# Summing the scan's states two pairs late, with a ninth state buffer, split rings for B and C, smaller loads of u and y, and a reordered opening

## The chip, the cores and the metric

The kernel runs on one core of a Trainium2 chip, in fp32. The metric is the device time of one execution in microseconds. The core has five engines that work side by side, each from its own queue in order: TensorE (PE), VectorE (DVE), ScalarE (ACT), GpSimd (POOL) and SyncE (SP), which here issues the DMAs.

## The reference

A sequence model of four layers runs on two sequences (b = 0, 1) of 1024 positions with 256 channels. Layer 0 is a Mamba block whose normalisation is shifted, scaled and gated by rows made from a condition vector. Layer 1 is a block of the same kind with two state-space models, of which the second runs backwards in time. Layer 2 is a linear attention, layer 3 a softmax attention, both with a shift and scale from the condition (FiLM). Most of the time goes into the state-space models, 512 channels with 16 states each:

```
def step(h, inp):
    dt_t, B_t, C_t, u_t = inp
    dA = jnp.exp(dt_t[:, :, None] * A)
    h = h * dA + (dt_t * u_t)[:, :, None] * B_t[:, None, :]
    y = jnp.einsum('bdn,bn->bd', h, C_t)
    return (h, y)
...
_, ys = jax.lax.scan(step, h0, seq)
y = jnp.transpose(ys, (1, 0, 2)) + u * D_param
y = y * jax.nn.silu(z)
```

There are six such recurrences: one for each sequence in layer 0, two for each in layer 1.

## The kernel before, in words

The order of instructions is written out by hand: the order of the program is the order on each engine's queue, and the tile pools add the waits for data and for buffers.

**The scans.** `chain()` runs the six recurrences one after the other in the order s00, s01, s10, s20, s11, s21 (layer, model, sequence as the code counts them). A tile holds 32 channels x 4 states on the 128 partitions and all 1024 positions; one recurrence has 64 tiles. They are taken in pairs that share four states (index k of 0 to 3): four blocks d of 128 channels, two halves cp of 64 channels, four k. That is 192 pairs p and 384 tiles, 2p and 2p+1. A tile takes these steps:

- `decay` (L133 as `dA_t<-sp`): ACT computes exp(A dt) from a spread of dt (`sp0`: 32 rows repeated four times by a DMA) into PSUM.
- `inputs` (L936): POOL multiplies the spread of dt*u (`sp1`) by B (`bc`, four rows repeated over 32 channels) into a state buffer `hb_t`. There are 8 of these buffers.
- `tile` (L943 backwards, L947 forwards): DVE runs the scan; then the result is multiplied by C, on DVE (L950), or for 99 of the 384 tiles on POOL (L949, called through `rest()`), whenever a running balance of the two engines' work says so.
- `fold` (L974): PE sums the four states of every channel into a bank `ys_t` by four matmuls for each tile. At k = 0 `begin` (L960, L964) opens the bank with u*D, and with the other direction's y where there are two.
- `finish` (L982): after four pairs the bank is multiplied by the gate on DVE, or copied by ACT, and stored by DMA.

In pair p the instructions come in this order: POOL's product for tile 2p+3, ACT's decay for 2p+1, a slot of other work, DVE's tile 2p, at k = 2 the finish of the group before, the gate's load at k = 3, the decay for 2p+2, the product for 2p+4, POOL's multiplication by C if there is one, a second slot, DVE's tile 2p+1, and at the end PE's sums for pair p-1:

```
            if p:
                fold(p - 1)
        fold(len(pairs) - 1)
```

The DMAs of the scans all go through SP's queue: `load_spread` (L899) fetches the spreads for the next group of pairs, three buffers for `sp0` and three for `sp1`; `load_bc` (L889) fetches B and C for one k into one ring of eight buffers, and for the next recurrence it is issued behind each of the last four pairs; `load_rest` (L913) fetches u and y for 128 channels into single buffers and makes a diagonal matrix of D; `load_gate` fetches the gate by 64 channels in two halves.

**The other work.** Everything else that the layers need (normalisation, projections, rows from the condition, the closing projection of each layer, the linear attention, the start of layer 3) is a queue of steps, `Behind`. `behind.slot()` is called twice for each pair and takes as many steps as its credits allow. `cond_later` is one of these steps: it makes the shift, scale and gate rows of layer 1 for both sequences, with matmuls (L95) and four POOL operations for each sequence. `until()` runs steps at once when a load needs their result.

**The opening.** Before the scans, the first sequence's preparation runs in the open: normalisation (`refine`, `scaled`), transposes with an eviction that applies the affine rows (`channels`), the projection into u and z, convolution, the projection to dt, B and C, and then the loads of the first scan. At the end of the scans, the softmax attention runs, from about 1476 us to the end.

Of the kernel before, what the change touches and what calls it, by code (L numbers as in the profile page):

```python
# [18 lines left out]
P = 128  # L19
# [18 lines left out]
for _name, _n in (  # L38
    ("ln_g0", 2), ("ln_b0", 2), ("ada_b0", 4), ("conv_w", 16), ("conv_b", 4),
    ("dt_b0", 4), ("D0", 4), ("Alog0", 64),  # L40
    ("n2g", 2), ("n2b", 2), ("bx", 4), ("bz", 4), ("bc1", 4), ("bc2", 4),
    ("dt_b1", 4), ("dt_b2", 4), ("D1", 4), ("D2", 4), ("Alog1", 64), ("Alog2", 64),
    ("ng2", 2), ("nb2", 2), ("bk2", 2), ("bv2", 2), ("emb_b2", 4), ("fg2", 2), ("fb2", 2),
    ("ng3", 2), ("nb3", 2), ("bq3", 4), ("bk3", 4), ("emb_b3", 4), ("fg3", 2), ("fb3", 2),
    ("mask3", 16), ("bq3d", 2), ("bk3d", 2), ("ones3", 2),
):
    _COLS[_name] = (_NCOLS, _n)
    _NCOLS += _n
# [6 lines left out]
def kernel(ctx: ExitStack, tc: tile.TileContext, a: dict, out: bass.AP):  # L55
# [5 lines left out]
    hbp = ctx.enter_context(tc.tile_pool(name="hbp", bufs=8))  # L61
# [141 lines left out]
    nc.scalar.preload_act_table_set("natural_log_exp_and_others")  # L203
# [49 lines left out]
    def affine(mod, scale_at, shift_at, g, bias, name):  # L253

        s = const.tile([P, 2, B], F32, tag=f"{name}s", name=f"{name}s")
        o = const.tile([P, 2, B], F32, tag=f"{name}o", name=f"{name}o")
        for c in range(2):
            g_c, b_c = col(g, c), col(bias, c)
            at = mod[:, scale_at + c, :]
            act_f(s[:, c, :], at, AF.Identity, bias=g_c, scale=g_c)  # L260
            t = small_t((P, B), "aff")
            act_f(t, mod[:, shift_at + c, :], AF.Identity, bias=b_c)
            for b in range(B):
                act_f(
                    o[:, c, b : b + 1], at[:, b : b + 1], AF.Identity,
                    bias=t[:, b : b + 1], scale=b_c,
                )
        return s, o
# [34 lines left out]
    def cond_later():  # L303
        scb = spread_cond()
        brow = abuf((1, 3 * D))
        nc.sync.dma_start(brow, a["ada_row1"])
        w = load_k("ada_w1", 3 * D)
        g1 = abuf((P, 2, D))
        nc.sync.dma_start(g1[:, 0, :], a["norm1_g"].partition_broadcast(P))
        nc.sync.dma_start(g1[:, 1, :], a["norm1_b"].partition_broadcast(P))  # L310
        yield 5 * T
        made = []
        yield from pipe(*(
            cond_rows(w, scb, brow, i * D, b, f"{name}1_{b}", res)
            for b in range(B)
            for i, (name, res) in enumerate(
                (("shift", made), ("scale", made), ("gate", cond["gate1"]))
            )
        ))
        for b in range(B):  # L320
            o, s = made[2 * b : 2 * b + 2]
            t = small_t((P, 2, D), "t2", 1)[:, 0, :]
            nc.gpsimd.tensor_scalar(s, s, 1.0, None, ALU.add)
            nc.gpsimd.tensor_tensor(t, s, g1[:, 1, :], ALU.mult)
            nc.gpsimd.tensor_tensor(o, o, t, ALU.add)
            nc.gpsimd.tensor_tensor(s, s, g1[:, 0, :], ALU.mult)
            cond["s1"].append(s)
            cond["o1"].append(o)
            yield
# [95 lines left out]
    def scaled(src, r, q):  # L425
        o = abuf((P, 4, D))
        for j in range(4 if mode["tail"] else 0):
            nc.vector.tensor_scalar(
                o[:, j, :], src[:, j, :], r[:, j : j + 1], q[:, j : j + 1], ALU.mult, ALU.add
            )  # L430
        for j in range(0 if mode["tail"] else 4):
            act_f(
                o[:, j, :], src[:, j, :], AF.Identity,
                bias=q[:, j : j + 1], scale=r[:, j : j + 1],
            )
        return o

    def normed(src, res):

        mv = small_t((P, 4 * len(src), 2), "mv", 4)  # L440
        for i, t in enumerate(src):
            stats(t, mv[:, ts(i, 4), :])
            yield
        r = root(mv)
        yield mode["least"] * 3 // 2
        q = refine(mv, r)
        yield
        for i, t in enumerate(src):
            res.append(scaled(t, r[:, ts(i, 4)], q[:, ts(i, 4)]))
            yield  # L450
# [7 lines left out]
    def channels(src, dst, func, scale, bias, halves=(0, 1)):  # L458


        def turn(i, c):
            ps = bank()
            for j in range(4):
                flip(ps[:, ts(j, P)], src[halves.index(i)][:, j, ts(c, P)])
            return ps

        def take(i, c, ps):
            act_f(
                dst[c][:, ts(i, 512)], ps, AF.Identity, bias=bias(c), scale=scale(c)
            )  # L470

        yield from pipe(*(
            (lambda i=i, c=c: turn(i, c), lambda ps, i=i, c=c: take(i, c, ps))
            for i in halves for c in range(2)
        ))
        if func is AF.Silu:
            done = slice(512 * halves[0], 512 * halves[-1] + 512)
            act_f(dst[0][:, done], dst[0][:, done], func)
            silu(dst[1][:, done])
            yield  # L480
# [75 lines left out]
    def ssm_inputs(key, u, w_xp, w_dt, dt_b, st):  # L556
# [15 lines left out]
        if key == "00":  # L572
# [7 lines left out]
            take(0, pss[0])  # L580
            nc.vector.tensor_copy(dbl[:, 512:], pss[1][: R + 2 * N, :])
# [5 lines left out]
        save(2, st["bc"], dbl[R : R + 2 * N, :])  # L587

# [287 lines left out]
    class Scan:  # L876
# [8 lines left out]
        def load_bc(self, k):  # L885
            for w in range(2):
                t = bcp.tile([P, T], F32, tag="bc", name="bc")
                at = w * N + k * NS
                nc.sync.dma_start(  # L889
                    t,  # L890
                    self.st["bc"][at : at + NS, :].unsqueeze(0).to_broadcast([DS, NS, T]),
                )
                self.bc[w][k] = t

        def load_spread(self, c, w):

            behind.until(lambda: len(self.st["have"]) > c // 4)
            t = spread.tile([P, T], F32, tag=f"sp{w}", name=f"sp{w}")
# [7 lines left out]
        def load_rest(self, d):  # L906
# [3 lines left out]
            self.rest[d] = {"D": diag(col(self.Dp, d), "dgD")}  # L910
            for key, src in srcs.items():
                t = fin.tile([P, T], F32, tag=f"f{key}", name=f"f{key}")
                nc.sync.dma_start(t, src[ts(d, P), :])  # L913
                self.rest[d][key] = t
# [5 lines left out]
        def load_gate(self, d, cp):  # L920
            if self.gate:
# [4 lines left out]
                self.rest[d]["g"] = t  # L926
# [7 lines left out]
        def inputs(self, c, k):  # L934
            e = hb()
            nc.gpsimd.tensor_tensor(e, self.sp[c, 1], self.bc[0][k], ALU.mult)  # L936
# [15 lines left out]
        def begin(self, d, cp):  # L952
# [3 lines left out]
            rest = self.rest[d]  # L956
            r = ts(cp, 64)
            for ch in range(2):
                o = self.ys[d, cp][ts(ch, 64), :]
                nc.tensor.matmul(  # L960
                    o, rest["D"][r, r], rest["u"][r, ts(ch, 512)], start=True, stop=False
                )
                if self.add is not None:
                    nc.tensor.matmul(  # L964
                        o, ident[r, r], rest["y"][r, ts(ch, 512)], start=False, stop=False
# [13 lines left out]
        def finish(self, d, cp):  # L979
            t = yp.tile([P, 512], F32, tag="y", name="y")  # L980
            if self.gate:
                nc.vector.tensor_tensor(t, self.ys[d, cp], self.rest[d]["g"], ALU.mult)  # L982
# [8 lines left out]
    def chain(scans, rates, early, mid, after):  # L991
# [29 lines left out]
        for w in range(2):  # L1021
            s.load_spread(0, w)
        s.load_bc(0)
        for w in range(2):
            s.load_spread(1, w)
        for k in range(1, NK):
            s.load_bc(k)
        s.load_rest(0)
        ahead(0, "decay")
        ahead(0, "inputs")  # L1030
# [5 lines left out]
        for p, (i, d, cp, k) in enumerate(pairs):  # L1036
# [10 lines left out]
            if k == 2 and cp == 1:  # L1047
                if d < 3:
                    s.load_rest(d + 1)
                elif nxt:  # L1050
                    nxt[0].load_rest(0)
# [25 lines left out]
            if k == 2 and nxt:  # L1077
                nxt[0].load_spread(nxt[1] + 1, 0)
# [7 lines left out]
            if final and i + 1 < len(scans):  # L1086
                scans[i + 1].load_bc(k)

            if p:
                fold(p - 1)  # L1090
        fold(len(pairs) - 1)
# [36 lines left out]
    def layer2(b, src, dst):  # L1128
# [110 lines left out]
        at = small.tile([P, 2, P], F32, tag="at", name="at", bufs=1)  # L1239
# [158 lines left out]
    def attention(sts, done):  # L1398
# [24 lines left out]
        def top(n, step, j, ps):  # L1423
            t, ch = divmod(step, 2)
            if n not in mh:
                mh[n] = small.tile([P, NT, 2, 4], F32, tag="mh", name="mh", bufs=2)
# [88 lines left out]
    ctx.enter_context(tc.manual_schedule())  # L1515
    sts = [{"v": [], "qk": [], "y": []} for _ in range(B)]
    with ExitStack() as s:
        bcp, spread, fin, yp = [
            s.enter_context(tc.tile_pool(name=n, bufs=k))
            for n, k in (("bcp", 8), ("spread", 3), ("fin", 1), ("yp", 2))  # L1520
        ]
        psum.append(s.enter_context(tc.tile_pool(name="psS", bufs=1, space=bass.MemoryType.PSUM)))
        s00 = Scan("00", negA[0], "D0", False, True)
        s01 = Scan("01", negA[0], "D0", False, True)
# [70 lines left out]
        for _ in range(7):  # L1595
            behind.step()
        behind.add(
            cond_first(), cond_later(), p01, p10, p20, cond_last(), p11, p21,
# [12 lines left out]
    home[0] = ctx.enter_context(tc.tile_pool(name="act2", bufs=17))  # L1611
    psum.append(ctx.enter_context(tc.tile_pool(name="psA", bufs=1, space=bass.MemoryType.PSUM)))
# [11 lines left out]
def _layout(i):  # L1624
# [16 lines left out]

    def heads(v, const_at=None):
# [11 lines left out]
        "dt_b0": cols(f["L0_cond_dt_proj_b"]), "D0": cols(f["L0_cond_D_param"]),  # L1654
# [5 lines left out]
        "D1": cols(f["L1_cond_Dp1"]), "D2": cols(f["L1_cond_Dp2"]),  # L1660
# [59 lines left out]
```

## Time and profile before

| | |
|---|---|
| median of 3 runs | 2124.39 us (2119.06 to 2125.03) |
| time of the profiled execution | 2117.43 us, its span 2115.4 us |
| first scan on DVE starts | 69.51 us |
| PE busy | 1626.8 us (77%), weight loads 617.7 us |
| DVE busy | 1745.5 us (83%) |
| ACT busy | 1140.4 us (54%) |
| POOL busy | 1356.9 us (64%) |
| POOL's products L936 | 384 at 2399 ns, 908.8 us |
| DVE's scans and products of L943 to L950 | 2279 to 2287 ns a scan, 1225 ns a product by C |
| PE's sums L974 | 1536 matmuls, 294.2 us |

How to read it: the busy shares are averages over a stretch of scans and a stretch of attention, in which other engines are full. In the scans one has to ask which of DVE and POOL is idle, and for whom. In the lines of waits, the engine and the line that waited stand ahead of the arrow and what released them behind it, with the total in us, the number of times and the longest. `hb_t` is a state buffer: a wait of POOL at L936 for PE is a wait for a buffer to come free.

### The profile page before, as it was taken

What the parts mean: (1) busy time and instruction counts of PE and PEld (TensorE: products, weight loads), DVE (VectorE), ACT (ScalarE), POOL (GpSimd) and SP (SyncE); (2) the same over time, 40 slices, a digit from 0 to 9 for tenths busy, and PEclk for the clock granted to TensorE, in tenths of its full rate; (3) what the DMA queues carried; (4) which work ended last, traced back from release to release, by engine and by line L of the source; (5) the groups of instructions that cost most, each with busy time, mean ns of one, the idle gap of its engine ahead of it and who ended that gap; (6) DMA issues with size and microseconds to landing.
All of it is one profiled execution on the core that took longest, in us unless ns stands there. A gap on an engine that the chain in (4) does not pass through costs nothing.

```text
span 2115.4 us, 22775 instructions
## 1 busy us (share of the span) xinstructions
PE 1626.8 (77%) x8112; PEld 617.7 (29%) x8112; DVE 1745.5 (83%) x1728; ACT 1140.4 (54%) x1583; POOL 1356.9 (64%) x667
## 2 busy tenths in 40 slices
PE   6576867288697547886945658944999899999997
PEld 3132313033141202222312323300545333333333
DVE  4688898898999999998999987998767757777763
ACT  5565666375546345764555453542044555656665
POOL 0789898898999999999998977998101211000000
PEclk9688968599796558988977865965899999999999
DMA  3663458245653555555653344332300111020001
GB/s 111 239 222 114 157 184 292 83 157 185 254 196 141 179 172 187 189 179 188 250 206 110 117 159 144 123 132 73 116 1 1 39 21 18 23 56 1 2 1 38
DMA packets 106870, 267.53 MB, mean 126 GB/s; under 512 B 14618, under 2 KB 39067, under 8 KB 106756
## 3 DMA queue, kind: packets, MB, share of 16 engines
q1 hardware_dynamic: 106756, 266.07, 37.1%
q8 instruction: 64, 1.05, 0.2%
q14 instruction: 50, 0.41, 0.1%
HBM read 195.90 MB, written 67.90 MB: 125 GB/s over the span
## 4 chain that ended last, share of the span: by engine, by line
PE 30%; DVE 10%; POOL 5%; issue 4%; ACT 2%; DMA 0%; DVEq 0%; ACTq 0%; POOLq 0%
PE sc_t L1418 13%; PE av_t L1458 6%; PE sc_t L95 4%; POOL hb_t L936 3%; PE bank_t L95 3%; DVE dA_t L943 2%; DVE mh L1427 2%; PE sc_t L99 2%; DVE dA_t L947 2%; POOL hb_t L949 1%; PE ys_t L974 1%; DVE hb_t L943 1%; ACT act_t L133 1%; POOL act_t L141 1%; DVE hb_t L947 1%
## 5 line engine op out<-in xcount | busy, mean ns | idle before, releaser
L936 POOL TENSOR_TENSOR hb_t<-sp,bc 128x1024 f32<-128x1024 f32 x384 | 908.8, 2399 | 88.5 <-PE ys_t L974 52.0
L133 ACT ACTIVATE dA_t<-sp,negA 128x1024 f32<-128x1024 f32 x384 | 428.5, 1117 | 548.3 <-DVE hb_t L950 432.8
L947 DVE TENSOR_TENSOR_SCAN dA_t<-dA_t,hb_t 128x1024 f32<-128x1024 f32 x195 | 445.9, 2287 | 62.3 <-ACT dA_t L133 35.1
L1427 DVE TENSOR_REDUCE mh<-sc_t 128x1 f32<-128x512 f32 x512 | 327.5, 686 | 110.2 <-PE sc_t L1418 109.8
L974 PE MATMUL ys_t<-hb_t,fold 128*32 128x512 f32 x1536 | 294.2, 781 | 153.5 <-POOL hb_t L949 101.1
L133 ACT ACTIVATE hb_t<-sc_t 128x512 f32<-128x512 f32 x512 | 276.9, 595 | 188.7 <-PE sc_t L1418 188.5
L950 DVE TENSOR_TENSOR hb_t<-dA_t,bc 128x1024 f32<-128x1024 f32 x285 | 349.1, 1225 | 21.4 <-DVE dA_t L947 0.5
L1418 PE MATMUL sc_t<-act_t 32*128 32x512 f32 x2048 | 336.6, 650 | 11.0 <-DVE mh L1427 7.3
L949 POOL TENSOR_TENSOR hb_t<-hb_t,bc 128x1024 f32<-128x1024 f32 x99 | 235.7, 2381 | 19.6 <-DVE hb_t L947 17.8
L784 POOL TENSOR_TENSOR act_t<-act_t,row 128x1024 f32<-128x1024 f32 x8 | 18.7, 2347 | 339.9 <-PE sc_t L99 193.3
L943 DVE TENSOR_TENSOR_SCAN dA_t<-dA_t,hb_t 128x1024 f32<-128x1024 f32 x90 | 205.7, 2285 | 9.2 <-POOL hb_t L936 6.0
L1458 PE MATMUL av_t<-hb_t,act_t 128*32 128x256 f32 x2048 | 164.3, 393 | 1.1 <-DVE act_t L1466 1.1
L95 PE MATMUL bank_t<-act_t,w_c_w 128*128 128x512 f32 x256 | 129.6, 657 | 41.2 <-ACT act_t L133 41.2
L133 ACT ACTIVATE act_t<-bank_t,cols 128x512 f32<-128x512 f32 (+1 forms) x206 | 129.9, 677 | 44.5 <-PE bank_t L95 38.7
L1418 PEld LDWEIGHTS sc_t<-act_t 32*128 32x128 f32 x2048 | 111.1, 185 | 120.9 <-issue 79.9
L974 PEld LDWEIGHTS ys_t<-hb_t,fold 128*32 128x32 f32 x1536 | 40.5, 123 | 358.9 <-POOL hb_t L949 139.5
L947 DVE TENSOR_TENSOR_SCAN hb_t<-dA_t,hb_t 128x1024 f32<-128x1024 f32 x61 | 139.0, 2279 | 3.9 <-ACT dA_t L133 3.6
L141 POOL TENSOR_TENSOR act_t<-act_t 128x1024 f32<-128x1024 f32 x50 | 118.4, 2367 | 0.2
L99 PE MATMUL bank_t<-ident,act_t 128*128 128x128 f32 x128 | 34.6, 426 | 92.5 <-ACT act_t L133 92.3
L95 PE MATMUL bank_t<-act_t,w_dt_w 64*128 64x512 f32 x96 | 74.6, 912 | 40.4 <-ACT act_t L133 34.4
L1458 PEld LDWEIGHTS av_t<-hb_t,act_t 128*32 128x32 f32 x2048 | 42.1, 108 | 190.5 <-issue 177.8
L1363 POOL MEMSET act_t<- 128x1024 f32 x8 | 7.6, 952 | 128.0 <-PE sc_t L1418 128.0
(176 smaller groups left out, 1833.9 us busy)
## 6 DMA issues: line engine op xcount, KB each, us to landing
sp<-dt SPq DMA_DIRECT2D x192, 512.0 KB, 5.3
dt<-act_t SPq DMA_DIRECT2D x48, 512.0 KB, 5.2
bc<-bc SPq DMA_DIRECT2D x48, 512.0 KB, 7.7
u<-act_t SPq DMA_DIRECT2D x24, 512.0 KB, 5.0
fu<-u SPq DMA_DIRECT2D x24, 512.0 KB, 4.5
y<-y SPq DMA_DIRECT2D x96, 128.0 KB, 5.8
g<-act_t SPq DMA_DIRECT2D x16, 512.0 KB, 5.3
fg<-g SPq DMA_DIRECT2D x64, 128.0 KB, 4.7
```

What stands on the lines that cost most here:

```text
L95: nc.tensor.matmul(o, w, x, **kw)
L133: nc.scalar.activation(o, x, func, **kw)
L141: nc.gpsimd.tensor_tensor(o, x, y, op)
L936: nc.gpsimd.tensor_tensor(e, self.sp[c, 1], self.bc[0][k], ALU.mult)
L943: nc.vector.tensor_tensor_scan(h[:, ::-1], dA[:, ::-1], e[:, ::-1], 0.0, ALU.mult, ALU.add)
L947: nc.vector.tensor_tensor_scan(h, dA, e, 0.0, ALU.mult, ALU.add)
L949: return lambda: nc.gpsimd.tensor_tensor(e, h, self.bc[1][k], ALU.mult)
L950: nc.vector.tensor_tensor(e, h, self.bc[1][k], ALU.mult)
L974: nc.tensor.matmul(self.ys[d, cp][at : at + DS, :], fold, e[:, ts(ch, 512)], start=False, stop=(k == NK - 1),)
L1418: nc.tensor.matmul(ps, w[r, ts(at, P)], x[r, ts(wide_at, 512)], start=True, stop=True)
L1427: nc.vector.tensor_reduce(mh[n][:, t, ch, j : j + 1], ps, AX.X, ALU.max)
L1458: nc.tensor.matmul(sums.av[32 * j : 32 * j + 32, ts(part, 256)], sts[b]["v"][t // 2][:, t % 2, 4 * g + j, :], es[j // 2][:, at : at + 256] ...
```

## The change

- The sums of a pair come two pairs later instead of one, and there are 9 state buffers instead of 8.
- The spreads of dt have four buffers instead of three. The first spread for the second tile's channels is issued at k = 1 instead of k = 2.
- B and C have a ring of four buffers each. For the next recurrence, B is issued ahead of the pair's first product, C behind the second tile.
- u and y are loaded for 64 channels, in two halves of 64 partitions x 512 positions, at every k = 3; before, for 128 channels at k = 2 of every second group. The diagonal of D is made for 64 channels (48 instead of 24 times).
- `cond_later` is split by sequence: the part for the second sequence runs after the preparation of s20, with its own load of the weights.
- The opening: half of the scalings, the affine rows and the second half of the evictions go from ACT to DVE; the copies of the dt, B, C projection are both on DVE; the first B is loaded right behind its store; the first product is on DVE; the order of the first loads is changed; the activation table is asked for behind the start of the hand-written order.
- Two small tiles share other tiles' memory.

```diff
-    hbp = ctx.enter_context(tc.tile_pool(name="hbp", bufs=8))
+    hbp = ctx.enter_context(tc.tile_pool(name="hbp", bufs=9))
...
     act_f(sc, cT, AF.Silu)
-    nc.scalar.preload_act_table_set("natural_log_exp_and_others")
...
             at = mod[:, scale_at + c, :]
+            if not mode["scans"]:
+                t = small_t((P, B), "aff")
+                nc.vector.tensor_scalar(t, at, 1.0, None, ALU.add)
+                nc.vector.tensor_scalar(s[:, c, :], t, g_c, None, ALU.mult)
+                nc.vector.scalar_tensor_tensor(
+                    o[:, c, :], t, b_c, mod[:, shift_at + c, :], ALU.mult, ALU.add
+                )
+                continue
...
-    def cond_later():
+    def cond_later(b):
         scb = spread_cond()
         brow = abuf((1, 3 * D))
         nc.sync.dma_start(brow, a["ada_row1"])
...
-    def scaled(src, r, q):
+    def scaled(src, r, q, i):
         o = abuf((P, 4, D))
-        for j in range(4 if mode["tail"] else 0):
+        far = mode["tail"] or i and not mode["scans"]
+        for j in range(4 if far else 0):
...
         def take(i, c, ps):
+            if c and not (mode["scans"] or mode["tail"]):
+                nc.vector.tensor_scalar(
+                    dst[c][:, ts(i, 512)], ps, scale(c), bias(c), ALU.mult, ALU.add
+                )
+                return
...
         save(2, st["bc"], dbl[R : R + 2 * N, :])
+        if "first" in st:
+            later(2, st["first"])
...
-        def load_bc(self, k):
-            for w in range(2):
-                t = bcp.tile([P, T], F32, tag="bc", name="bc")
...
+        def load_bc(self, k, w):
+
+            t = bcp.tile([P, T], F32, tag=f"bc{w}", name=f"bc{w}")
...
-            t = spread.tile([P, T], F32, tag=f"sp{w}", name=f"sp{w}")
+            t = spread.tile([P, T], F32, tag=f"sp{w}", name=f"sp{w}", bufs=4 - w)
...
-            self.rest[d] = {"D": diag(col(self.Dp, d), "dgD")}
+            rest = self.rest[d, cp] = {"D": diag(col(self.Dp, 2 * d + cp), "dgD")}
             for key, src in srcs.items():
-                t = fin.tile([P, T], F32, tag=f"f{key}", name=f"f{key}")
-                nc.sync.dma_start(t, src[ts(d, P), :])
-                self.rest[d][key] = t
+                rest[key] = t = fin.tile([P, 512], F32, tag=f"f{key}", name=f"f{key}")
+                for ch, half in enumerate(self.halves(src, d, cp)):
+                    nc.sync.dma_start(t[ts(ch, 64), :], half)
...
-        for w in range(2):
-            s.load_spread(0, w)
-        s.load_bc(0)
-        for w in range(2):
-            s.load_spread(1, w)
+        for c in range(2):
+            for w in range(2):
+                s.load_spread(c, w)
+        s.load_bc(0, 1)
         for k in range(1, NK):
-            s.load_bc(k)
-        s.load_rest(0)
+            for w in range(2):
+                s.load_bc(k, w)
+        s.load_rest(0, 0)
         ahead(0, "decay")
-        ahead(0, "inputs")
+        made["inputs"][0] = s.inputs(0, 0, nc.vector)
         ahead(1, "inputs")
         ahead(2, "inputs")
...
-            if k == 2 and cp == 1:
-                if d < 3:
-                    s.load_rest(d + 1)
-                elif nxt:
-                    nxt[0].load_rest(0)
+            if k == 1 and nxt:
+                nxt[0].load_spread(nxt[1] + 1, 0)
+            if final and i + 1 < len(scans):
+                scans[i + 1].load_bc(k, 0)
+            if k == 3 and nxt:
+                nxt[0].load_rest(nxt[1] // 4, nxt[1] // 2 % 2)
             ahead(2 * p + 3, "inputs")
...
-            if k == 2 and nxt:
-                nxt[0].load_spread(nxt[1] + 1, 0)
             ahead(2 * p + 4, "inputs")
...
             if final and i + 1 < len(scans):
-                scans[i + 1].load_bc(k)
-
-            if p:
-                fold(p - 1)
-        fold(len(pairs) - 1)
+                scans[i + 1].load_bc(k, 1)
+
+            if p > 1:
+                fold(p - 2)
+        for p in (2, 1):
+            fold(len(pairs) - p)
...
-            ("bcp", 8), ("spread", 3), ("fin", 1), ("yp", 2)
+            ("bcp", 4), ("spread", 3), ("fin", 1), ("yp", 2)
...
-            cond_first(), cond_later(), p01, p10, p20, cond_last(), p11, p21,
+            cond_first(), cond_later(0), p01, p10, p20, cond_later(1), cond_last(), p11, p21,
```

## The prediction

> **What bounds the kernel now.** I read the profile in four steps: the busy time by stage, the waits of VectorE (DVE) and GpSimd (POOL) inside the scans, the waits of the engines that feed them, and the first 70 us one instruction at a time. All sums stand against the profiled execution: 2117.43 us with a span of 2115.4 us. The median of the runs shown is 2124.39, 7.0 above it (2119.06 to 2125.03).
>
> By stage (length, busy us and instructions of PE, PE weight load, DVE, ACT, POOL, then the granted PE clock, the DMA share and GB/s):
>
> ```profile
> 85.00:150.00 65.00, 42.97 (x143) 15.82 (x141) 55.97 (x33) 41.35 (x44) 57.66 (x25) 0.81 0.58 203
> 150.00:300.00 150.00, 117.21 (x375) 40.98 (x375) 129.48 (x89) 98.15 (x131) 140.11 (x73) 0.82 0.44 146
> 600.00:750.00 150.00, 109.42 (x385) 42.24 (x386) 142.64 (x95) 77.02 (x98) 149.09 (x65) 0.67 0.44 154
> 1200.00:1350.00 150.00, 113.27 (x409) 52.15 (x410) 126.45 (x111) 71.50 (x95) 116.70 (x70) 0.69 0.42 145
> ```
>
> The scans run from the first at 69.5 us to the last at 1472.6 us, and the attention behind them is not touched. In the scans two engines are nearly full at once: from 600 to 1200 us DVE is idle only some 7 to 8 us in 150 and POOL at most 9. DVE idles beyond that floor in just two stretches: 37 us from 85 to 600 and 16 us from 1200 to 1350. So about 53 us is all that better feeding can win in the scans, and the stretch ahead of 69.5 us is the other place. The reader is to see that neither a faster ACT nor a faster PE is worth anything by itself.
>
> What the two full engines wait for, and what feeds them (us in all, times, longest):
>
> ```profile
> DVE dA_t L947 <- ACT dA_t L133: 35.1, 18, 4.7
> DVE act_t L791 <- PE bank_t L95: 24.5, 7, 7.9
> DVE dA_t L947 <- POOL hb_t L936: 13.2, 10, 3.9
> POOL hb_t L936 <- PE ys_t L974: 52.0, 20, 12.3
> POOL hb_t L949 <- DVE hb_t L947: 17.8, 5, 8.4
> POOL hb_t L936 <- DMA bc<-bc: 12.5, 4, 4.4
> ACT dA_t L133 <- DMA sp<-dt: 27.5, 6, 7.0
> PE ys_t L974 <- POOL hb_t L949: 101.1, 25, 8.4
> PE ys_t L974 <- DVE hb_t L950: 52.4, 21, 7.1
> ```
>
> POOL's largest wait is for a state buffer that PE has not yet summed (52.0). PE stands 153 us at sums whose state isn't ready; that matters only where other PE work queued behind it is wanted.
>
> The opening (start, duration, instruction, and in brackets the idle time before it):
>
> ```profile
> 14.23 4.05 ACT L133 ACTIVATE act_t<-act_t,newt,rstd 128x256 f32<-128x256 f32 x8 [0.83 <-DVE newt L422]
> 20.51 1.43 ACT L133 ACTIVATE act_t<-bank_t,aff0o,aff0s 128x512 f32<-128x512 f32 x2
> ...
> 67.14 2.34 POOL L936 TENSOR_TENSOR hb_t<-sp,bc 128x1024 f32<-128x1024 f32 x1 [10.15 <-DMA bc<-bc]
> 69.51 2.30 DVE L947 TENSOR_TENSOR_SCAN dA_t<-dA_t,hb_t 128x1024 f32<-128x1024 f32 x1 [13.65 <-POOL hb_t L936]
> ```
>
> ACT's eight scalings stand ahead of the first eviction at 20.51, and the first scan waits for POOL, which waits for B.
>
> **The change, part by part.**
>
> *Opening, front.* Four of ACT's eight scalings go to DVE (0.44 us each there by the same operation in the attention, 0.59 on ACT), the twelve small affine operations become six on DVE at about 0.17 to 0.2 (its small operations of that stage take 165 ns). ACT drops 4 x 0.59 + 2.3 (18.18 to 20.51). DVE's own line, four scalings and six small ones, ends near 18.2, and the first eviction follows there instead of at 20.51: −2.4. Between PE and conv nothing else changes. The move of the table-set preload: two table loads of 1.28 us stand in the trace, at 10.28 and 11.89, and in the new order both loads still stand ahead of their functions, so I take 0. The rule in the Trainium skill ("ScalarE: Activation LUTs", section "Table sets: the hidden batching unit") says ln and exp sit together in one set, so that one load serves; by it the sum would be 1.28 us lower. I go with the order of instructions.
>
> *Opening, first scan.* B's first load is issued behind its own store, ahead of dt's, so it has landed when dt's spread lands; the first product runs on DVE (1.25 us by the row 1225 ns) instead of POOL (2.34). The spread should land near 63.5 to 64, and the scan start near 65.5 instead of 69.5; but C is now fifth in SP's queue and POOL's next product starts only when spread and B are both there (about 66.9 instead of 70.87). Net −3 to −3.5. Opening together: **−6**, bounds −9 and −2.
>
> *B and C in two rings.* B of the next scan is issued one tile earlier, in its own ring. It can take away POOL's 12.5 us for B, which fall at the starts of scans (4.2, 4.4, 3.5 us). POOL sets the pace at some of these places: **−4** (0 to −12.5).
>
> *Fourth spread for dt.* ACT waits for spreads 27.5 us (about 24 of it in running scans), but DVE behind it waits only 2.4 and 2.2 us at two scan starts. **−4** (0 to −24): a little more than those two, as ACT's evictions also come earlier. The load goes ahead of other loads on SP at k = 1; SP's queue waits for POOL's release of the other spread 644 us in total, so an early wait on SP costs those queued behind it, gate and sum loads with pairs of lead. I price that at 0, and up to 5 if the lead is gone.
>
> *Sums two pairs late.* PE then meets states that POOL finished a pair ago: the 153 us of stalls mostly go. What stood behind them is what counts. In the last stage before attention, the larger part of the stalls has nothing on PE behind it. DVE's L791 waits for PE's bank 24.5 us, ACT's evictions 15.3 (150 to 300) and 10.0 (450 to 600). **−6** (0 to −15).
>
> *Its costs.* A state buffer is held a pair longer and there is only one buffer more. The product for tile 2p+4 waits at the same point of PE as before, that for 2p+3 now one pair's sums later. I laid the recorded end of each pair's sums beside the recorded start of each odd product: 57 of 188 would come late, by 2.7 us each, 154 us in total. Beyond the lead that these products have before their own scan only 2.6 us is left, but POOL is itself full: **+3** (0 to +30). The finish of a group (L979) stays where it was while the group's last sum comes a pair later: by the recorded times 0.4 to 2.5 us late at a few of 48 groups; DVE shows just 2.0 us of such waiting today: **+4** (0 to +10).
>
> *Rows for the second batch made late.* 15 matmuls (about 8 us of PE) and four POOL operations (3.0 us) leave the first scan, where DVE has its largest excess idle time, and come back behind the third scan's preparation with a second load of the weights (4 x 384 KB, 6.7 us each, far ahead of use). **−2** (−4 to +3).
>
> *u and y by 64 channels.* 24 more diagonals at 392 ns are 9.4 us of ACT, which has 548 us of idle before its decays; 96 transfers of 128 KB stand where 24 of 512 KB stood for u, and 32 where 8 stood for y. The nearest row is the gate's 128 KB load, 4.7 us to landing, against 4.5 us for 512 KB: two of them side by side are 4.7. The skill's rule speaks against this ("DMA: Bandwidth & Descriptors", section "Rules for kernel authors": two transfers to disjoint partition halves serialize, one transfer over 128 partitions is to be used): by it 9.4 us. The load has three pairs, some 21 us, before its use, so by either it is hidden: 0 on the path, and with ACT's diagonals and the second set of rows **+2** (0 to +6). If the lead were gone it would cost 4.7 us by the rule at up to 48 groups.
>
> *Order of the other layers' steps.* They come two tiles earlier up to tile 80 and eight tiles later from tile 172 on; they all end before the scans do: 0 (−10 to +10).
>
> Sum: −6 −4 −4 −6 +3 +4 −2 +2 = **−13**, that is 2104 against the profiled 2117.4, and 2111 against the median. I put the likeliest time between, at **2107**.
>
> **The rivals.** *The feed was the limit (larger gain).* The idle beyond the floor goes together: spreads, B, sums and rows hit the same 85 to 600 us. Of 37 + 16 some 33 goes, with −6 of the opening: −39, with the costs at their low end, to about 2080, at best 2072. For it: these four remedies each name a wait in exactly those stages. Against: DVE's waits put down to the causes the change touches are far fewer than 53 us.
>
> *It does not do what it says (no change).* PE's waits at the sums were cover, not cost; a buffer is freed no earlier, and with a pair more of delay the one buffer more just balances. The opening's 6 is eaten by the +3, +4 and +2 and by the steps that come later: 2124. For it: POOL's 52 us for buffers come from PE's other work, and that stays.
>
> *Slower: POOL becomes the pacer through late buffers.* Nine buffers serve the products ahead and two pairs awaiting sums. POOL's lead is two tiles, 4.7 us; where PE comes to the end of a pair's sums later than that, behind another layer's matmuls (PE is 117 of 150 us busy in one stage), POOL starts late and, having no slack (149.1 busy of 150 us from 600 to 750), never makes it up. It decides once a fifth of the 154 us, 31 us, goes into POOL's pace; with the opening's −6 that is +25 and more by the profile, about 2142. For it: POOL already waits 52 us on just this. Against: the leads worked out above absorb all but 2.6 us.
>
> **How the numbers follow.** This kernel's measurement can tell about 0.3%, 6.4 us, from no change: faster is below 2118.0, slower above 2130.8. The forecast, 2107 with an own range of 2098 to 2117, has 0.50; the larger gain 0.18; no change 0.14; slower 0.18. So faster 0.68, same 0.14, slower 0.18. The range of 2072 to 2137 leaves out the last part of the slower case (about 0.13) and little of the larger gain (0.05).
>
> **What would show it.** Right: the first scan near 65 us; POOL's wait for B gone from the scans; ACT's wait for spreads gone; PE's 153 us at the sums mostly gone; DVE idle down by 7 to 15 us between 85 and 600 us. The costs would show as a larger POOL wait for PE at L936's successor and a new DVE wait for PE at the finish. Wrong: POOL's wait for PE over 80 us with DVE's wait for POOL over 40 (the slower case), or DVE at the idle floor from 150 us on (the larger gain); or a stretch of attention that differs by more than 3 us, which I hold untouched.

## The result and the profile after

The changed kernel takes 2144.62 us (median of 8 runs, 2130.41 to 2147.8) against 2122.08 us for the kernel before, by now also with 8 runs: a ratio of 1.0106, with a 95% interval of 1.0077 to 1.0135. It is slower by some 22 us where the forecast was 2107 us, and it lies above the range's end of 2137. It is the slower rival that came, with nearly the time that it named (2142).

The profiled execution of the changed kernel took 2130.41 us with a span of 2128.7 us, the fastest of the eight. Against the profiled execution before, its loss is 13 us; so the trace shows the kinds of loss, and the ratios of the runs their size.

The stages, in the columns of the first fence of the prediction:

```profile
85.00:150.00 65.00, 42.05 (x154) 17.83 (x158) 59.46 (x35) 44.78 (x51) 58.96 (x26) 0.84 0.61 215
150.00:300.00 150.00, 107.37 (x328) 35.71 (x320) 121.85 (x84) 96.41 (x125) 130.40 (x66) 0.80 0.46 150
600.00:750.00 150.00, 106.99 (x390) 42.95 (x390) 142.83 (x84) 78.11 (x93) 145.10 (x66) 0.73 0.44 152
1200.00:1350.00 150.00, 94.94 (x406) 50.35 (x402) 134.22 (x122) 71.15 (x98) 123.66 (x73) 0.75 0.42 137
```

In the stage from 150 to 300 us, DVE works 7.6 us less than before (121.85 against 129.48) and POOL 9.7 less (130.40 against 140.11). This was the stage that was to win. From 85 to 600 us together, DVE is busy 443.5 of 515 us instead of 451.8: its idle time rose by 8 us, where a fall of 7 to 15 was forecast.

The waits of the two full engines and of PE in the scans of the changed kernel (us in all, times, longest):

```profile
DVE y L997 <- PE ys_t L989: 22.6, 11, 3.4
DVE dA_t L962 <- POOL hb_t L951: 17.7, 17, 2.4
DVE dA_t L958 <- POOL hb_t L951: 15.9, 13, 3.3
DVE dA_t L962 <- ACT dA_t L133: 14.0, 10, 3.6
POOL hb_t L951 <- PE ys_t L989: 81.5, 27, 8.0
POOL hb_t L951 <- DMA bc<-bc: 0.6, 1, 0.6
PE ys_t L989 <- POOL hb_t L964: 81.8, 17, 9.7
PE ys_t L989 <- DVE hb_t L965: 21.9, 8, 5.8
PE bank_t L95 <- ACT act_t L133: 138.9, 48, 12.1
PE bank_t L99 <- ACT act_t L133: 125.5, 12, 22.5
```

L951 is the product of L936, L989 the sum of L974, L997 the finish of L982. Three lines carry the loss. POOL waits 29.5 us longer for buffers (81.5 against 52.0); DVE, behind it, waits 33.6 us for products instead of 19.2; and a new wait of 22.6 us stands at the finish of a group. The last two lines say where PE's time went. In the trace before they were:

```profile
PE bank_t L95 <- ACT act_t L133: 103.5, 43, 12.6
PE bank_t L99 <- ACT act_t L133: 89.0, 11, 15.3
```

PE's stalls at the sums fell by 50 us (153.5 to 103.7), and its stalls at the other layers' matmuls rose by 72 us (192.5 to 264.4; in the first experiment below, which puts back the sums alone, they are 199.6). A sum that stands two pairs later in PE's queue stands behind two more slots of other work. PE did not get freer by that: it stood in front of another instruction, with the sums queued behind it. From the end of a pair's last operation on DVE to the start of its sums on PE, the median is 6.3 us in the trace before and 12.4 us in the trace after. The state buffers are held those 6.1 us longer, for one buffer more. While POOL waits those 81.5 us, PE runs matmuls of other layers for 44 us of them.

The opening came as described. The timeline of the changed kernel:

```profile
17.42 0.78 ACT L133 ACTIVATE act_t<-bank_t,aff0o,aff0s 128x512 f32<-128x512 f32 x1 [1.09 <-PE bank_t L99]
...
62.43 1.23 DVE L951 TENSOR_TENSOR hb_t<-sp,bc 128x1024 f32<-128x1024 f32 x1 [8.49 <-DMA sp<-dt]
63.76 2.30 DVE L962 TENSOR_TENSOR_SCAN dA_t<-dA_t,hb_t 128x1024 f32<-128x1024 f32 x1
65.54 2.37 POOL L951 TENSOR_TENSOR hb_t<-sp,bc 128x1024 f32<-128x1024 f32 x1 [10.48 <-DMA sp<-dt]
```

The first eviction starts at 17.42 instead of 20.51 and the first scan at 63.76 instead of 69.51. This lead of 5.8 us is gone by the scan of tile 48 (2.1 us late), and the last scan starts 11.8 us late, at 1484.4. The attention takes 1.5 us longer than before.

### The profile page after: what moved, and what is told of

It reads as the page before. It is cut to its first block, busy times and chain, and to the rows that moved or that the text cites. A ratio compares the mean times of both kernels' runs of the same rounds, so it can differ in the third digit from the quotient of the medians.

```text
span 2128.7 us, 22977 instructions
## 1 busy us (share of the span) xinstructions
PE 1605.3 (75%) x8112; PEld 620.5 (29%) x8112; DVE 1749.8 (82%) x1742; ACT 1143.2 (54%) x1593; POOL 1358.2 (64%) x666
## 5 line engine op out<-in xcount | busy, mean ns | idle before, releaser
L951 POOL TENSOR_TENSOR hb_t<-sp,bc 128x1024 f32<-128x1024 f32 x383 | 908.2, 2398 | 113.2 <-PE ys_t L989 81.5
L989 PE MATMUL ys_t<-hb_t,fold 128*32 128x512 f32 x1536 | 257.1, 728 | 103.8 <-POOL hb_t L964 81.8
L798 POOL TENSOR_TENSOR act_t<-act_t,row 128x1024 f32<-128x1024 f32 x8 | 19.2, 2401 | 340.8 <-DMA act_t<-x 340.8
L1433 PEld LDWEIGHTS sc_t<-act_t 32*128 32x128 f32 x2048 | 111.3, 187 | 121.3 <-issue 79.4
L989 PEld LDWEIGHTS ys_t<-hb_t,fold 128*32 128x32 f32 x1536 | 37.5, 119 | 280.3 <-POOL hb_t L964 111.8
L95 PE MATMUL bank_t<-act_t 128*128 128x256 f32 (+5 forms) x160 | 64.8, 568 | 37.7 <-DMA act_t<-in_ada_w 26.8
```

What stands on the lines that cost most here:

```text
L95: nc.tensor.matmul(o, w, x, **kw)
L951: engine.tensor_tensor(e, self.sp[c, 1], self.bc[0][k], ALU.mult)
L989: nc.tensor.matmul(self.ys[d, cp][at : at + DS, :], fold, e[:, ts(ch, 512)], start=False, stop=(k == NK - 1),)
L1433: nc.tensor.matmul(ps, w[r, ts(at, P)], x[r, ts(wide_at, 512)], start=True, stop=True)
```

## The experiments

Each ratio is to the kernel before, run on the same chip, with its 95% interval. The twelve experiments were run in three groups of four, in the order below, each group on another chip; a comparison across groups takes it for granted that such a ratio carries over from chip to chip, which was not tried. The two runs of the changed kernel with eight buffers share a group, so that comparison stands without it. I call the condition "one late" or "two late" by the distance of the sums.

**One late again.** The changed kernel with this edit:

```diff
-            if p > 1:
-                fold(p - 2)
-        for p in (2, 1):
-            fold(len(pairs) - p)
+            if p:
+                fold(p - 1)
+        fold(len(pairs) - 1)
```

> The changed kernel with PE's sums one pair late again; nine buffers and all else stay. Theory (the later sums themselves cost: state buffers come back a pair later and the finish of a group meets an unfinished sum): DVE's wait for PE at the finish falls from 20.6 us to under 4, POOL's wait for PE's sums from 81.5 to under 45, DVE's wait for POOL's products from 33.5 to under 20; time about 2115, ratio to the kernel before about 0.997 (0.990 to 1.002). Rival (the order of the other layers' steps, the second load of weights and the smaller DMAs cost, and the sums only show it): ratio stays at 1.006 to 1.012.

Measured: 0.9947 (0.9929 to 0.9964). The loss is gone and more; the second pair of distance costs 0.0159, some 34 us. Its waits:

```profile
POOL hb_t L951 <- PE ys_t L989: 8.9, 7, 3.8
DVE y L997 <- PE ys_t L989: 2.0, 1, 2.0
PE ys_t L989 <- POOL hb_t L964: 127.2, 33, 8.2
PE ys_t L989 <- DVE hb_t L965: 60.9, 22, 8.5
PE bank_t L95 <- ACT act_t L133: 114.1, 42, 13.4
PE bank_t L99 <- ACT act_t L133: 85.5, 11, 15.7
```

The wait at the finish falls from 22.6 us to 2.0 and POOL's wait for PE from 81.5 to 8.9, and PE's stalls at the sums are back, at 188 us, without harm. DVE's wait for products fell only from 33.6 to 26.4 us, not under 20. The theory holds.

**The finish a pair later.**

```diff
-            ended = pairs[p - 3][:3] if p > 2 and k == 2 else None
+            ended = pairs[p - 4][:3] if p > 3 and k == 3 else None
```

> The changed kernel with the finish of a group one pair later (k = 3 instead of 2), so that it again has the old distance from its last sum. Theory: the 20.6 us of DVE's wait at the finish go, POOL's wait for buffers stays near 80: ratio about 1.002 (0.999 to 1.005), half of the loss won back. Rival (what the finish stops waiting for, DVE then waits for at POOL's products, since POOL is the pacer): ratio 1.008 to 1.012, DVE's wait for POOL's products grows from 33 to 45 or more.

Measured: 1.0056 (1.0034 to 1.0078), between the two expectations. The wait at the finish is gone, 22.6 us, and DVE's wait for products grew from 33.6 to 46.2 (29.5 and 16.7), so about half of it only changed its name. POOL's wait for PE is 70.5 us. What is left is a gain of 0.005, 11 us, with an interval of about 8.

**Ten buffers.** Ten state buffers in the scans, nine in the attention, and to pay for the space three spreads of dt, loaded at k = 2.

```diff
-    hbp = ctx.enter_context(tc.tile_pool(name="hbp", bufs=9))
+    hbp = []
...
+        hbp.append(s.enter_context(tc.tile_pool(name="hbp", bufs=10)))
...
-            t = spread.tile([P, T], F32, tag=f"sp{w}", name=f"sp{w}", bufs=4 - w)
+            t = spread.tile([P, T], F32, tag=f"sp{w}", name=f"sp{w}", bufs=3)
...
```

> The changed kernel with ten state buffers in the scans (nine in the attention) and, to pay for it, three spreads of dt loaded at k = 2 as before. Theory: POOL's wait for PE falls from 81.5 to near the 52 of before, DVE's wait for POOL's products from 33.5 to under 20, the finish keeps its 20; ACT's wait for spreads comes back (24 us, little of it on DVE): ratio about 1.003 (1.000 to 1.007). Rival: no change at all from the changed kernel (1.008 to 1.012), as POOL's waits were slack.

Measured: 0.9949 (0.9926 to 0.9972), below what was expected. Its waits:

```profile
POOL hb_t L951 <- PE ys_t L989: 50.2, 19, 6.2
DVE y L997 <- PE ys_t L989: 19.2, 9, 3.3
```

POOL's wait is where it was before the change, and DVE's wait for products is down from 33.6 to 14.1 us. The wait at the finish stays, and still the kernel is as fast as with sums one late and nine buffers.

**Both.** Finish a pair later and ten buffers.

> The finish one pair later and ten buffers together, sums still two late. Theory: both costs of the later sums are gone and their gain (PE free for the other layers' matmuls) remains: ratio about 0.995 (0.989 to 1.000). Rival: the rest of the change costs, 1.003 or more.

Measured: 0.9937 (0.9917 to 0.9957), 0.0012 below ten buffers alone, which is within the intervals. The theory's 0.995 was met.

**Three spreads, nine buffers.** The control of the run with ten buffers.

```diff
-            t = spread.tile([P, T], F32, tag=f"sp{w}", name=f"sp{w}", bufs=4 - w)
+            t = spread.tile([P, T], F32, tag=f"sp{w}", name=f"sp{w}", bufs=3)
...
-            if k == 1 and nxt:
-                nxt[0].load_spread(nxt[1] + 1, 0)
...
+            if k == 2 and nxt:
+                nxt[0].load_spread(nxt[1] + 1, 0)
```

> The changed kernel (nine buffers, sums two late) with three spreads of dt loaded at k = 2 as before: the control of the run with ten buffers, which had both. Theory (the tenth buffer won the 35 us): ratio stays at 1.007 to 1.014, POOL's wait for PE near 80 us. Rival (the fourth spread's earlier load was what cost, by standing in SP's queue): ratio falls to 0.995 to 1.001.

Measured: 1.0089 (1.0061 to 1.0116). The fourth spread was not what cost; between nine and ten buffers, with all else equal, lie 0.0140, some 30 us. POOL's wait for PE is 79.4 us here and 50.2 with ten.

**Eight buffers.** The changed kernel with `bufs=8`.

> The changed kernel with eight state buffers, sums two late: the dose on the other side. Theory (the number of buffers against the distance of the sums sets POOL's waits): from nine to ten it won about 35 us, so from nine to eight it costs more than that: ratio 1.03 to 1.07, POOL's wait for PE above 150 us and DVE's wait for POOL's products above 80. Rival (the finish or the other work costs): ratio under 1.018.

Measured: 1.0408 (1.038 to 1.0437). The dose works in this direction too, and its waits grow with it:

```profile
POOL hb_t L951 <- PE ys_t L989: 149.9, 41, 8.5
DVE dA_t L962 <- POOL hb_t L951: 66.7, 46, 4.8
DVE dA_t L958 <- POOL hb_t L951: 20.3, 16, 3.1
```

**One late and eight buffers.** Both as before the change, the rest as changed.

> The changed kernel with sums one pair late and eight buffers, as both were before; the rest of the change stays. Against the run with nine buffers and one late (0.995) it tells what the ninth buffer is worth there. Theory: one buffer for each pair of distance less would be balanced, so about as the kernel before but for the opening and the rings: ratio 0.996 to 1.003, POOL's wait for PE back to 30 to 60 us. Rival (the ninth buffer is idle with sums one late): 0.993 to 0.996.

Measured: 0.9972 (0.9959 to 0.9985). The ninth buffer is worth 0.0025 here, 5 us, at the edge of what the intervals can tell. POOL's wait for PE is 38.8 us, within the forecast.

**The opening alone**, in the kernel before, with the edits of the opening as the diff above shows them.

> The kernel before with the changed opening alone. Theory: the first scan starts near 63.8 us instead of 69.5 and the lead is kept to the end: ratio 0.9973 (0.9955 to 0.999). Rival (a head start is lost again in the first scans, since POOL and the loads there do not come earlier): ratio 0.999 to 1.002.

Measured: 0.9954 (0.9938 to 0.9969), about 10 us. In its trace the first scan starts at 62.6 us, 6.9 earlier, and this head start shrinks to 1.9 us by tile 320, so the trace does not show it kept to the end. Over the next eight tiles it grows to 16.9 us; the last section looks at that stretch.

**One late and ten buffers**, with three spreads.

> The changed kernel with sums one pair late, ten buffers and three spreads of dt loaded at k = 2: beside the run with ten buffers and sums two late (0.995) it tells what the later sums are worth where their buffers are paid for. Theory (the later sums win nothing themselves, since PE's stalls at the sums were cover): 0.992 to 0.997, the same within the interval, DVE's wait for PE at the finish gone. Rival (PE free for the other layers' matmuls was worth about 6 us, as forecast): 0.997 to 1.001.

Measured: 0.9895 (0.9868 to 0.9922), median 2092.68 us. This beats both kernels and is the fastest of all runs. It is below the theory's range: beside the run with ten buffers and sums two late, which was made on another chip, the later sums lose 0.0054, some 11 us, even where the buffers are paid for. The wait at the finish is 2.0 us in this run and was 19.2 with sums two late. From nine to ten buffers the ratio falls from 0.9940 (the next run) to 0.9895, though POOL's wait for PE falls only from 10.2 to 4.0 us; that gain is not explained.

**One late, nine buffers, three spreads.**

> The changed kernel with sums one late, nine buffers, and three spreads of dt loaded at k = 2: what the fourth spread is worth, against 0.995 with four. Forecast (4 us of gain from the fourth): 0.9965. Rival (ACT's waits for spreads were cover): 0.994 to 0.996, with ACT's wait for spreads back at 20 us or more and DVE's wait for ACT unchanged within 5 us.

Measured: 0.994 (0.9914 to 0.9965) against 0.9947 with four spreads. ACT waits 17.5 us for spreads instead of 6.3, DVE's largest wait for ACT is 24.1 instead of 23.4. DVE does not wait longer for that; the forecast of 4 us is not seen, in either pair of runs.

**The rows together**, one late, eight buffers.

```diff
-            cond_first(), cond_later(0), p01, p10, p20, cond_later(1), cond_last(), p11, p21,
+            cond_first(), cond_later(), p01, p10, p20, cond_last(), p11, p21,
```

> Sums one late, eight buffers (0.997 in the run before), and the condition's rows for both sequences made together in the first scan, as before the change. Forecast (the split is worth 2 us): 0.998. Rival (the split costs, by its second load of weights and the later order of steps): 0.993 to 0.996. The scan of tile 48 should start 2 to 6 us later than with the split if the first scan is relieved by it.

Measured: 0.9927 (0.9899 to 0.9956), against 0.9972 with the split. By these two runs, which were made on two chips, the split costs 0.0045, some 10 us with an interval of 7, where I had forecast a gain of 2. The scan of tile 48 starts at 244.2 us, 4 us earlier than with the split (248.2), not later. DVE's wait for products is also smaller over the whole scans (16.8 us against 26.3). Why the first scan gets quicker with more work in it isn't settled: the order of all the steps behind it shifts too, and no run holds that fixed.

**The kernel before with sums two late**, eight buffers, nothing else.

> The kernel before with nothing changed but the sums, two pairs late with its eight buffers. Theory: the loss is that of the changed kernel with eight buffers (1.041) without the opening's gain: 1.045 (1.038 to 1.055), POOL's wait for PE near 150 us. Rival (the changed kernel's other parts made the sums late, such as its smaller loads of u and y in front of the sums): under 1.03.

Measured: 1.0539 (1.0505 to 1.0572), 113 us more (2229.6 against 2116.44). The one edit is enough.

```profile
POOL hb_t L936 <- PE ys_t L974: 165.5, 45, 12.6
DVE dA_t L947 <- POOL hb_t L936: 55.4, 38, 3.6
DVE dA_t L943 <- POOL hb_t L936: 27.2, 18, 3.1
```

DVE's wait for products, 19.2 us in the kernel before, is 82.6 by the last two lines. ACT's wait for spreads rose too, from 27.5 us to 93.6; how much of the loss that carries isn't known.

The runs give a table of sums against buffers (* with three spreads of dt, which changes nothing that can be measured with nine buffers):

| buffers | one late | two late | difference |
|---|---|---|---|
| 8 | 0.9972 | 1.0408 | 0.0436 |
| 9 | 0.9947, 0.9940* | 1.0106, 1.0089* | 0.0159, 0.0149* |
| 10 | 0.9895* | 0.9949* | 0.0054 |

The order of the program explains the rows. A tile's buffer is that of the tile n before it, n being the number of buffers, and a pair holds two. With ten buffers and sums two late, both products of pair p therefore wait for the sums issued at the same places of PE's queue as with eight buffers and sums one late: the product for tile 2p+3 for those at the end of pair p-2, the one for tile 2p+4 for those at the end of pair p-1. With nine buffers both wait for the end of pair p-1. The two balanced runs lie at 0.9949 and 0.9972, with 50.2 and 38.8 us of POOL's wait for PE.

The loss of the change can be followed in steps, each between two measured kernels: the opening −0.0046, the rings, spread, rows, smaller loads and shared tiles together +0.0018, the ninth buffer −0.0025, the sums two late +0.0159; in all +0.0106. In us of 2122: −9.8, +3.8, −5.3, +33.7, in all +22.4.

## Why the prediction was wrong, point by point

**The late buffers, +3 (0 to +30): this is the step that failed.** The working found that 57 of 188 products would come late, 154 us in all, and then let the lead of the products take up all but 2.6 us. Both figures come out of the recorded times again. But each late product was set against the whole lead that it had in a trace where POOL waited 52 us, as if the lead were there anew each time; POOL, busy 149.1 of 150 us, has little idle time to win it back. The traces show it shrink: from the end of a product to the start of its scan, the median is 4.8 us before, 3.6 us in the changed kernel, 1.7 us in the kernel before with nothing but the sums two late, 4.8 us again with ten buffers. POOL's wait for PE rose by 29.5 us, a fifth of the 154, just where the slower rival said that it decides. The step from nine to ten buffers is worth about 30 us, the upper bound that I had set. I had named the right mechanism and priced it by the wrong end. For the later sums with both of their costs the forecast had −6 +3 +4, that is +1 us; the runs gave +34. With +34 in that place the forecast's sum is +20 instead of −13, and the measured change is +22.

**The sums two late, −6.** Wrong in kind. I counted PE's stalls of 153 us as time that mostly goes; a third of them went, and more came back at the other layers' matmuls, which stand in the same queue. With ten buffers the later sums still cost 0.0054, so a gain from them is seen in none of the three pairs of runs. DVE's wait for PE at L791 did fall from 24.5 to 10.2 us in the changed kernel, but it is just as small with sums one late (9.2 with eight buffers), so this wasn't the sums' doing.

**The finish, +4 (0 to +10).** In kind right, too small: 22.6 us of waiting, of which moving the finish wins 11 back. At ten buffers, the two ways of taking the wait away do not agree well: the later finish wins 0.0012, sums one late 0.0054, and the intervals of about 0.003 allow both to be the same. How much of the 0.0054 is the finish is thus open.

**The opening, −6.** Right at the first scan, which came 5.8 us earlier, at 63.76; the first eviction came at 17.42 rather than the 18.2 forecast. What it is worth at the end is less clear. The runs of the opening alone gave 10 us, with an interval of 3. But the traces do not show the head start kept: it is gone by tile 48 in the changed kernel and down to 1.9 us by tile 320 with the opening alone, and what comes there behind tile 320 was not forecast. That the total has the size of the forecast is in part luck. The two table loads stayed, as taken:

```profile
10.31 1.28 ACT L133 ACT_TABLE_LOAD   x1 [5.08 <-DVE mv L401]
11.92 1.28 ACT L133 ACT_TABLE_LOAD   x1
```

The rule in the Trainium skill ("ScalarE: Activation LUTs", section "Table sets: the hidden batching unit") would have had one of them. Here there are two in both traces, one ahead of the logarithm and one ahead of the exponential. The request for the joint set, which the change moves in the program, runs at 0.78 us in both, and a load for another function follows at 3.69 and 3.72.

**B and C, −4.** POOL's wait for B is gone from the scans (12.5 to 0.6 us). What it is worth alone was not run. Between the opening alone (0.9954) and the run with the rows together (0.9927) lie rings, spread, smaller loads and shared tiles: −0.0027 with an interval of about 0.003, on two chips. It agrees with −4 us and with nothing.

**The fourth spread, −4.** Nothing: 0.9947 against 0.9940 and 1.0106 against 1.0089, within the intervals. ACT's wait for spreads did go (27.5 to 2.3 us). DVE's waits behind it were 2.4 and 2.2 us, in all 4.6, so −4 was not "a little more than those two" but a little less, and I should have taken 4.6 as the upper bound, not near the middle.

**The rows, −2.** Wrong sign, as far as two chips can be compared: they cost about 10 us. The cause isn't settled.

**Smaller loads of u and y, 0 on the path.** Not tried alone. They landed in 2.8 us each (median of the 25 landings that the trace has, 128 KB), so two of them, even one after the other as the rule of the Trainium skill ("DMA: Bandwidth & Descriptors", "Rules for kernel authors") has it, need some 5.6 us of the 21 us of lead. In the seven pairs of which the trace has both landings, the second was issued 0.5 us after the first and landed 0.6 us after it (medians), 4.0 us after the first was issued: they were under way together, and the trace does not show them one after the other. SP stood 94 us for the release of their single buffers (56.7 and 37.7), while PE waited 0.4 us for u.

**The chances.** The evidence for the slower rival was in the text: POOL busy 149.1 of 150 us, and already 52 us of waits for just these buffers. Of its two signs one came in full (POOL's wait for PE over 80: 81.5) and one in part (DVE's wait for POOL over 40: 33.6, with 22.6 more at the finish). The static working, 2.6 us beyond the lead, was a lower bound.

## What to carry to other kernels

Moving an instruction later in an in-order queue did not free the engine from waiting here; it put other waits in front of it, and all that it releases came later. Count buffers together with the distance between the producer and the instruction that frees them: a pair holds two, so one more pair of distance asked for two more buffers, and with one it lost 34 us. Price a lead by what remains when the engine that lives off it has no idle time to win it back.

## What the runs showed of the hardware

In one stretch, the granted clock of PE differs by about a factor of two between traces. The stretch follows the scan of tile 320 at the same distance, first in the trace of the kernel before and then with the opening alone (columns as in the first fence of the prediction); by that scan PE has started 1424 matmuls other than those of the scans in both, and by the scan of tile 328 it has started 1488:

```profile
1265.00:1285.00 20.00, 20.00 (x45) 9.85 (x43) 7.68 (x6) 6.36 (x7) 10.80 (x5) 0.50 0.48 164
```

```profile
1263.00:1283.00 20.00, 16.46 (x72) 7.95 (x71) 17.05 (x22) 8.04 (x9) 19.76 (x9) 1.00 0.77 249
```

With a clock of 0.50 PE is full and gets 45 matmuls done, DVE works 7.7 of 20 us; with 1.00 it does 72 and DVE works 17.1. The eight tiles from 320 on took 47.2 us in the one and 32.3 in the other: 15 of the 17 us between the two profiled executions come from here. DVE waits for PE at L791 for 17.5 us in the one case and 2.6 at its successor in the other, so what DVE waited for at L791 in the trace before, 24.5 us, was in good part this. Two more traces have the same count of matmuls there: the kernel before with sums two late was slow too (46.6 us, clock 0.55), the rows together were fast (32.8 us, clock 0.97). Both slow ones have the old opening and both fast ones the new, so four traces can't tell whether this is chance or an effect of the opening, and of the opening's 10 us it may be the larger part.

In the trace of the first experiment (2116.05 us, 4 above the median of its runs) a single instruction lost 13 us. DVE's conversion of 128x1024 int32 to fp32 at L1150 took 14.27 us while POOL ran six operations without a pause. The 14 traces hold this instruction and its twin in the attention 28 times. In the 14 cases in which POOL was not within an operation when it started, it took 0.67 or 0.68 us. In the 14 in which POOL was, it ended 0.54 or 0.55 us behind the end of an operation of POOL: mostly of the one then running, in the one long case of the last of the six. So beside a POOL that is nearly full, this short instruction can be held up long; why it is let through between two operations in some cases and not in others isn't shown.
